# A two-layer graph kernel: the last product as seven products of halves, in a new order of steps

## The chip, the cores and the metric

The kernel runs on one core of a Trainium2 chip. The metric is the device time of one launch in microseconds (us), the median of three runs; the profile is taken by the hardware profiler in one further execution.

## The reference, cut to what matters

There are 128 graphs of 128 nodes with 512 features (`x`, f32) and a 0/1 adjacency `adj`. Two layers follow each other; each normalizes, runs an attention over the nodes of its graph and adds the result to `x`. Layer 0 has eight heads of 64, layer 1 four heads of 64. The change is in the end of layer 1:

```
# layer 0
h = relu(layernorm(x))
m = h @ map_w.T + map_b               # heads n = m / |m| per head
q = m @ q_w.T + q_b ; k = m @ k_w.T + k_b
adj0 = (n n^T > 0.1) * softmax(mask(q k^T / 8))
x = x + relu((adj0 @ (h @ gcn_map_w.T + gcn_b)) @ gcn_W.T / (adj0.sum + 1))
# layer 1
h = relu(layernorm(x))
q, k, v = h @ Wq, h @ Wk, h @ Wv      # 512 -> 256
o = softmax(mask(q k^T / 8)) @ v      # 128 x 256 per graph
x = x + o @ Wo + bo                   # 256 -> 512
```

All arithmetic is f32.

## The kernel before

**Blocks and turns.** Two graphs make a block (`G = 2`, 64 blocks). Each block goes through some forty steps, methods of `Block`. Their order is written out by hand in two lists. `TURN` (lines 934 to 1074) is one turn of the loop at line 1473: an entry `(back, step, ...)` runs the step on block `turn - back`, so that one turn works on blocks in several stages: loads and the first normalization three and two blocks ahead (back -3, -2, -1), the products of layer 0 on the block itself (0), its scores and attention one turn later (1), the mix and the products of layer 1 two turns later (2), the scores of layer 1 (3), and the last mix and the output product (4). `TAIL` (1078 to 1368) holds what is left of the last blocks; there `(back, ...)` means block 64 - back. Each engine executes its instructions in the order of these lists; waits between engines come from the data and from the reuse of buffers. For the turns before turn 2 a variant `early` of the list moves one step, `halves` of layer 0, to a place ahead of `unit 0` (lines 1469 to 1471).

**Products by halves.** The big products multiply the features of both graphs by a weight matrix. A weight matrix is cut into four blocks, the activations of the two graphs into four quarters, and instead of eight products of blocks, seven are made (`p`, lines 375 to 414), with sums of activations (`halves`, S1 to S4, on POOL; on DVE in layer 1 for the last two blocks, where `late` is true) and sums of weights made once. The seven write into three PSUM banks X, Y and Z: products 1 and 2 into X, 6, 7 and 4 into Y, 5 and 3 into Z. Between them the banks are read: `r` copies X after product 1, `u 1` reads Y after product 6, `u 2` reads Y after product 7, `c` reads a bank into the destination. So product 7 waits for `u 1`, product 4 for `u 2`, product 3 for `c 1 1`, which reads Z after product 5. The kinds are `qk` and `ms` (layer 0) and `qk1` and `v` (layer 1). `ms` streams 512 columns in each matmul, `qk`, `qk1` and `v` 128. Every f32 matmul shows as two records of PE.

**The output product.** It is not made in this way: `project(g)` (910 to 921) takes the two 128x128 pieces of `oT` (one graph's `o`, turned) as stationary operand and streams the 512 columns of `w_o1`, so four matmuls of 512 columns in a block, and `project_out` (923 to 926) adds the bank to `x1` on DVE; `store` writes `x1` out. `x1` is the block's x of layer 1 with the bias `b_o` already in it (`bias1`, POOL).

**PE's modes.** The scores use 64 rows of the array (`scores0`, `near`, `scores1` through line 557; called *row steps* below), the mixes 64 columns (`mix0` line 692, `mix1` line 892; *column steps*), the products the full array. A turn's PE steps before, with [back]:

```
mix0 0[2], mix1[4], mix0 1[2] | scores0 0[1], scores0 1[1] | p qk 1, 6, project 1[4],
p qk 2, 7, project 0[4], p qk 5, 4, 3 | scores1[3], near 1[1], near 0[1] | p ms 1, 6, 5,
p qk1 1[2], p ms 7, 2, 4, 3, p qk1 6, p v 1, 6, p qk1 7, 2, 5, p v 2, 7, p qk1 4, 3, p v 5, 4, 3
```

**Other steps that are named below.** `mix0_out` (DVE) divides the mix, `residual` adds it to x (POOL; DVE when late), `stats1`, `rstd`, `norm1` normalize (DVE, POOL, ACT), `h1`, `h1_put`, `h1_get`, `h1_out` turn the result by way of DRAM (late: by PE transposes), `squares`, `norms`, `unit`, `nT` make the unit heads (ACT, DVE, POOL, DVE), `h0_out` (ACT) writes `hT`, the input of the next block's products. `scores0_out`, `max0`, `near_out`, `scores1_out` are DVE, `exps0`, `exps1`, `near_T_out`, `mix1_out` are ACT.

Of the kernel before, what the change touches and what calls it, by code (L numbers as in the profile page):

```python
# [8 lines left out]
F32 = mybir.dt.float32  # L9
# [11 lines left out]
def kernel(  # L21
# [53 lines left out]
    w_o1 = const.tile([P, IC, D], F32, name="w_o1")  # L75
    b_ms = const.tile([P, 2, D], F32, name="b_ms")
    b_d = const.tile([P, D], F32, name="b_d")
# [146 lines left out]
    class Block:  # L224
# [130 lines left out]
        def quarters(self, layer):  # L355
            h = self.h1T if layer else self.hT
            return [[h[:, g, 2 * k : 2 * k + 2, :] for k in range(2)] for g in range(G)]

        def halves(self, layer):
            A = self.quarters(layer)  # L360
            add = (nc.vector if self.late and layer else nc.gpsimd).tensor_tensor
            tag = f"halves{layer}"
            t = keep1.tile([P, 4, 2, S], F32, tag=tag, name=f"{tag}_{self.b}")
            S1, S2, S3, S4 = (t[:, i] for i in range(4))
# [13 lines left out]
        def p(self, kind, i):  # L378
            layer = int(kind in ("qk1", "v"))
# [12 lines left out]
            if kind in ("ms", "v"):  # L392
                for c in range(2):
                    rhs = (w_ms if kind == "ms" else w_v1)[:, w, c, :]
# [5 lines left out]
                        stop=(c == 1),  # L400
# [16 lines left out]
        def dest(self, kind, g, half):  # L417
# [4 lines left out]
            if kind == "v":  # L422
                if "v1" not in f:
                    f["v1"] = keep2.tile([P, G, INNER], F32, tag="v1", name=f"v1_{b}")
                return f["v1"][:, g, half * P : (half + 1) * P]
            n = KC if kind == "qk" else IC
# [5 lines left out]
        def shaped(self, kind, t):  # L432
            if kind == "ms":
                return t.rearrange("p (k h d) -> p k h d", k=2, d=DK)
            if kind == "v":
                return t[:, :P]
            t = t.rearrange("p (c t) -> p c t", t=S)
# [4 lines left out]
        def r(self, kind, i):  # L442
            X = self.f[kind, "X"]
            if kind in ("qk1", "v"):
# [6 lines left out]
            if i == 1 and kind == "ms":  # L451
                nc.vector.tensor_add(r, X, b_ms[:, 1])
            elif i == 1:
# [5 lines left out]
            elif kind == "ms":  # L459
                nc.gpsimd.tensor_tensor(  # L460
                    self.f[kind, tag],
                    self.f[kind, "r1"],
                    self.shaped(kind, b_d),
                    ALU.add,
                )
# [8 lines left out]
        def u(self, kind, i):  # L474
            Y = self.shaped(kind, self.f[kind, "Y"])
            nc.vector.tensor_add(self.dest(kind, i - 1, 1), Y, self.f[kind, "r1"])  # L476

        def c(self, kind, g, half):
            bank = self.shaped(kind, self.f[kind, ("XZ", "YZ")[g][half]])
            out = self.dest(kind, g, half)  # L480
            if half:
# [428 lines left out]
        def project(self, g):  # L910
            b = self.b
            py = mm_bank(f"py_{b}_{g}")
            for c in range(IC):
                nc.tensor.matmul(  # L914
                    py,
                    lhsT=self.f["oT"][:, g, c, :],
                    rhs=w_o1[:, c, :],
                    start=(c == 0),
                    stop=(c == IC - 1),
                )  # L920
            self.f["py", g] = py

        def project_out(self, g):
            b = self.b
            y = self.x1[:, g, :]
            nc.vector.tensor_add(y, self.f["py", g], y)
# [8 lines left out]
        (2, "mix0", 0),  # L935
        (4, "mix1"),
        (2, "mix0", 1),
        (2, "mix0_out", 0),
        (2, "residual", 0),
        (1, "scores0", 0),  # L940
        (4, "mix1_out"),
        (1, "nT_put"),
        (1, "scores0", 1),
        (2, "mix0_out", 1),
        (2, "residual", 1),
        (0, "p", "qk", 1),
        (2, "stats1", 0),
        (2, "rstd", 1, 0),
        (1, "scores0_out", 0),
        (0, "r", "qk", 1),  # L950
        (2, "stats1", 1),
        (2, "norm1", 0),
        (0, "p", "qk", 6),
        (4, "project", 1),
        (2, "rstd", 1, 1),
        (0, "p", "qk", 2),
        (1, "max0", 0),
        (0, "u", "qk", 1),
        (0, "p", "qk", 7),
        (4, "project", 0),  # L960
        (1, "nT_get"),
        (2, "norm1", 1),
        (-2, "stats0", 1),
        (2, "bias1", 0),
        (2, "h1"),
        (0, "p", "qk", 5),
        (2, "h1_put"),
        (1, "scores0_out", 1),
        (0, "r", "qk", 2),
# [559 lines left out]
```

## Time and profile before

| | before |
|---|---|
| median of three runs | 3009.96 us (3009.82 to 3010.53) |
| the profiled execution, its own time | 3010.06 us |
| its span in the trace | 3008.3 us |
| mean granted TensorE clock | 0.999 |
| one turn in the steady state | 45.71 us |
| steady turns (4 to 62), start to end of the stretch | 199.3 to 2896.1 us |

A turn's length is read off the timeline of PE: the first scores of a turn start at 202.21, 247.92, 293.63 us and so on. In the lists of the profile, a line of a group gives line, engine, operation, output<-input, shapes and count, then busy time, mean ns of one, and idle time before it with what ended it. In a timeline, the columns are start (us), duration (us), engine, line, operation and count; an instruction's duration holds the drain of the pipeline, so a group's cost is the start of the next group minus its own start.

### The profile page before, as it was taken

The numbers are of one execution on the slowest core, as the hardware profiler recorded it, in microseconds if no ns is written. First come the engines' busy times: TensorE is split into PE (matmuls) and PEld (weight loads), VectorE is DVE, ScalarE is ACT, GpSimd is POOL, SyncE is SP. The second block draws the span as 40 slices with busy tenths as digits, with TensorE's granted clock in tenths as the row PEclk, the third lists the DMA queues.
The fourth block names the chain that finished last, engine by engine and source line by source line (L and its number), as shares of the span: only waits on it lengthen the run. The fifth ranks groups of instructions, "written<-read, shape, count | busy, mean of one in ns | idle before, by whom it ended". The sixth has DMA issues, their size and how long they took to land.

```text
span 3008.3 us, 68541 instructions
## 1 busy us (share of the span) xinstructions
PE 2986.0 (99%) x25336; PEld 2367.4 (79%) x25336; DVE 2418.2 (80%) x4586; ACT 1469.3 (49%) x4637; POOL 1750.9 (58%) x2423
## 2 busy tenths in 40 slices
PE   8999999999999999999999999999999999999999
PEld 5787787787787887877877877877878878778777
DVE  3788888888888888888888888888888888888877
ACT  2454554554544544545545545545445445455444
POOL 1566566566565565665665665655655656656642
PEclk9999999999999999999999999999999999999999
DMA  4356565565565565565555664664655655655542
GB/s 156 97 172 184 158 189 178 155 190 179 151 193 177 154 187 176 167 184 165 181 183 155 187 181 152 189 183 148 191 177 159 185 172 173 184 159 187 173 139 76
DMA packets 304109, 507.33 MB, mean 169 GB/s; under 512 B 49184, under 2 KB 180512, under 8 KB 295840
## 3 DMA queue, kind: packets, MB, share of 16 engines
q1 hardware_dynamic: 301072, 502.39, 54.8%
q8 instruction: 201, 3.29, 0.4%
q10 hardware_dynamic: 2704, 0.57, 0.1%
q14 instruction: 132, 1.08, 0.1%
HBM read 273.20 MB, written 229.64 MB: 167 GB/s over the span
## 4 chain that ended last, share of the span: by engine, by line
PE 97%; DVE 1%; DMA 1%; POOL 0%; issue 0%; ACT 0%; ACTq 0%; SPq 0%; DVEq 0%; POOLq 0%
PE py_qk L407 17%; PE px_qk L407 11%; PE pz_qk L407 11%; PE py_ms L395 11%; PE px_ms L395 8%; PE pz_ms L395 7%; PE py L914 7%; PE po L692 4%; PE psc L557 4%; PE pc L557 4%; PE py_v L395 3%; PE ps L557 2%; PE pz_v L395 2%; PE px_v L395 2%; PE po L892 2%; PE pw_k L132 0%
## 5 line engine op out<-in xcount | busy, mean ns | idle before, releaser
L617 ACT ACTIVATE s<-s,mx 128x128 f32<-128x128 f32 x1024 | 396.4, 393 | 73.0 <-DVE mx L603 73.0
L513 POOL TENSOR_TENSOR rn<-rn,mhalf 128x8 f32<-128x8 f32 x128 | 212.9, 1663 | 331.7 <-DVE rn L508 259.5
L407 PEld LDWEIGHTS py_qk<-halves,w_qk 128*128 128x128 f32 x3072 | 368.9, 192 | 32.8 <-issue 31.8
L407 PEld LDWEIGHTS pz_qk<-halves,w_qk 128*128 128x128 f32 x3072 | 368.2, 192 | 29.4 <-issue 28.7
L407 PE MATMUL py_qk<-halves,w_qk 128*128 128x128 f32 x3072 | 387.3, 276 | 2.3 <-DVE kT L476 2.2
L407 PE MATMUL pz_qk<-halves,w_qk 128*128 128x128 f32 x3072 | 385.0, 275 | 0.4 <-DVE halves L365 0.4
L407 PEld LDWEIGHTS px_qk<-hT,w_qk 128*128 128x128 f32 x2048 | 243.9, 192 | 39.7 <-issue 32.3
L365 POOL TENSOR_TENSOR halves<-h1T 128x256 f32<-128x256 f32 x62 | 45.0, 726 | 381.2 <-ACT h1T L318 381.2
L407 PE MATMUL px_qk<-hT,w_qk 128*128 128x128 f32 x2048 | 256.5, 279 | 3.5 <-DVE mix L713 3.5
L815 ACT ACTIVATE s<-s,mx 128x128 f32<-128x128 f32 x496 | 192.9, 390 | 136.2 <-DVE mx L802 136.2
L395 PE MATMUL px_ms<-w_ms,hT 128*128 128x512 f32 x512 | 247.1, 605 | 0.0
L914 PE MATMUL py<-w_o,oT 128*128 128x512 f32 x512 | 240.9, 594 | 0.9 <-DVE oT L905 0.9
L395 PE MATMUL py_ms<-w_ms,halves 128*128 128x512 f32 x512 | 240.7, 592 | 0.0
L395 PE MATMUL pz_ms<-w_ms,halves 128*128 128x512 f32 x512 | 240.6, 592 | 0.0
L318 ACT ACTIVATE hT<-mv 128x1024 f32<-128x1024 f32 x64 | 67.7, 1057 | 318.1 <-PE py_ms L395 318.1
L456 ACT ACTIVATE r_qk<-px_qk,b_k 128x128 f32<-128x128 f32 x256 | 73.2, 369 | 271.1 <-PE px_qk L407 271.1
L724 POOL TENSOR_TENSOR x<-x,mix 128x512 f32<-128x512 f32 x124 | 157.3, 1269 | 71.2 <-DVE mix L713 55.7
L617 ACT ACTIVATION_READ_ACCUMULATOR s<-s,mx 128x1 f32 x1024 | 197.1, 193 | 0.0
L851 POOL TENSOR_TENSOR s<-s,z 128x512 f32<-128x512 f32 x124 | 126.3, 1040 | 118.6 <-DVE z L844 118.6
L395 PEld LDWEIGHTS pz_ms<-w_ms,halves 128*128 128x128 f32 x512 | 97.2, 190 | 122.0 <-issue 107.4
L395 PEld LDWEIGHTS px_ms<-w_ms,hT 128*128 128x128 f32 x512 | 91.9, 189 | 98.9 <-issue 91.4
L395 PEld LDWEIGHTS py_ms<-w_ms,halves 128*128 128x128 f32 x512 | 92.5, 190 | 92.8 <-issue 92.5
(151 smaller groups left out, 7196.1 us busy)
## 6 DMA issues: line engine op xcount, KB each, us to landing
d_h<-hn SPq DMA_DIRECT2D x504, 128.0 KB, 3.7
mv<-d_h SPq DMA_DIRECT2D x126, 512.0 KB, 4.3
d_near<-s SPq DMA_DIRECT2D x248, 256.0 KB, 3.8
near_mv<-d_near SPq DMA_DIRECT2D x62, 1024.0 KB, 5.4
xt<-in_x SPq DMA_DIRECT2D x64, 512.0 KB, 7.2
x<-in_x SPq DMA_DIRECT2D x64, 512.0 KB, 6.3
out<-x SPq DMA_DIRECT2D x128, 256.0 KB, 2.3
d_n<-n SPq DMA_DIRECT2D x248, 128.0 KB, 3.0
```

The source lines that it names most:

```text
L318: nc.scalar.activation(t.rearrange("p g c (a j) -> p (g c) a j", a=Q), self.f.pop((key, "moved")).rearrange("p a r j -> p r a j"), func,)
L395: nc.tensor.matmul(bank[:, : rhs.shape[1]], lhsT=src[:, c, :], rhs=rhs, start=(first and c == 0), stop=(c == 1), skip_group_check=True,)
L407: nc.tensor.matmul(bank[:, oc * P : (oc + 1) * P], lhsT=(w_qk1 if layer else w_qk)[:, w, c, oc * P : (oc + 1) * P], rhs=src[:, c, :], star ...
L456: nc.scalar.activation(r[:, cols], X[:, cols], AF.Identity, bias=b_k[:, oc : oc + 1])
L513: nc.gpsimd.tensor_tensor(rn, rn, mhalf[:, :H0], ALU.pow)
L557: nc.tensor.matmul(dst[par][:, :, first + step * p, :], lhsT=lT(rows, p), rhs=rT(rows, p), start=True, stop=True,)
L617: nc.scalar.activation(s[:, :, g, par, c, :], s[:, :, g, par, c, :], AF.Exp, bias=mx[:, i : i + 1], accum_out=z[:, h : h + 1],)
L692: nc.tensor.matmul(po[h // PR][half * DK : (half + 1) * DK, h % PR, :], lhsT=f["nearT", g][:, (h % 2) * PR + h // 2, half * DK : (half + 1 ...
L724: (nc.vector if self.late else nc.gpsimd).tensor_add(x1, x1, self.f["mix", g])
L815: nc.scalar.activation(s[:, :, par, c, g, :], s[:, :, par, c, g, :], AF.Exp, bias=mx[:, par, c, g : g + 1], accum_out=z[:, par, c, g : g + 1],
L851: nc.gpsimd.tensor_tensor(s[:, :, par].rearrange("p q c g j -> p q (c g) j"), s[:, :, par].rearrange("p q c g j -> p q (c g) j"), z[:, par ...
L914: nc.tensor.matmul(py, lhsT=self.f["oT"][:, g, c, :], rhs=w_o1[:, c, :], start=(c == 0), stop=(c == IC - 1),)
```

## The change

The product with `w_o` becomes a fourth user of the seven products (kind `y`, "layer" 2): the quarters are the 128x128 pieces of `oT`, the weight blocks 128x256, and each product is one matmul of 256 columns. `halves 2` makes the four sums of `oT` (POOL; DVE when late) in the buffer that `halves 1` uses; `r y` copies product 1 to SBUF (ACT); `first_to_x1` adds that copy to the three quarters of `x1` that need it (POOL, 128x256 and 128x512); then two `u` and four `c` add the banks to quarters of `x1` in place (DVE, 128x256 each). `project` and `project_out` go. `w_o1` is loaded by four transfers instead of one, and its four sums are made by DVE in the first turns, where the pieces of such work (`one_piece`) are now also spread over the `qk` steps. The constant `b_d` goes; `r ms 2` becomes two POOL additions over contiguous operands instead of one. Both lists have a new order. The turn's PE steps after it:

```
mix0 0[2], mix0 1[2], mix1[4] | scores0 0[1] | p qk 1, 6 | scores0 1[1], scores1[3] |
p qk 2, 7, 5, 4, 3 | near 1[1], near 0[1] | p ms 1, p y 1[4], p ms 6, 5, p y 6, p ms 7,
p y 5, 7, 2, p qk1 1[2], p ms 2, p y 3, 4, p ms 4, 3, p qk1 6, p v 1, 6, 5, p qk1 7, 5,
p v 7, p qk1 2, p v 2, p qk1 4, p v 3, p qk1 3, p v 4
```

`h0_out` now stands after `squares 1` and `unit 0`, and in the early turns `halves` of layer 0 stands behind `h0_out`, and so behind `unit 0`. `nT_put` moves from the next turn to the end of its own.

The diff, its two lists cut:

```diff
@@ -72,9 +72,8 @@
     w_qk = const.tile([P, 7, 2, D], F32, name="w_qk")
     w_qk1 = const.tile([P, 7, 2, INNER], F32, name="w_qk1")
     w_v1 = const.tile([P, 7, 2, INNER // 2], F32, name="w_v1")
-    w_o1 = const.tile([P, IC, D], F32, name="w_o1")
+    w_o1 = const.tile([P, 7, 1, D // 2], F32, name="w_o1")
     b_ms = const.tile([P, 2, D], F32, name="b_ms")
-    b_d = const.tile([P, D], F32, name="b_d")
     b_o = const.tile([P, D], F32, name="b_o")
     b_q = const.tile([P, KC], F32, name="b_q")
     b_k = const.tile([P, KC], F32, name="b_k")
@@ -353,15 +352,18 @@
 
 
         def quarters(self, layer):
+            if layer == 2:
+                return [[self.f["oT"][:, g, k : k + 1, :] for k in range(IC)] for g in range(G)]
             h = self.h1T if layer else self.hT
             return [[h[:, g, 2 * k : 2 * k + 2, :] for k in range(2)] for g in range(G)]
 
         def halves(self, layer):
             A = self.quarters(layer)
             add = (nc.vector if self.late and layer else nc.gpsimd).tensor_tensor
-            tag = f"halves{layer}"
-            t = keep1.tile([P, 4, 2, S], F32, tag=tag, name=f"{tag}_{self.b}")
-            S1, S2, S3, S4 = (t[:, i] for i in range(4))
+            t = keep1.tile(
+                [P, 4, 2, S], F32, tag=f"halves{min(layer, 1)}", name=f"halves{layer}_{self.b}"
+            )
+            S1, S2, S3, S4 = (t[:, i, : 1 if layer == 2 else 2] for i in range(4))
             add(S1, A[1][0], A[1][1], ALU.add)
             add(S2, S1, A[0][0], ALU.subtract)
             add(S3, A[0][0], A[1][0], ALU.subtract)
@@ -376,7 +378,7 @@
 
 
         def p(self, kind, i):
-            layer = int(kind in ("qk1", "v"))
+            layer = {"qk1": 1, "v": 1, "y": 2}.get(kind, 0)
             A = self.quarters(layer)
             S = self.f.get(("S", layer))
             nm, src, w, first = (
@@ -389,15 +391,17 @@
                 ("Y", S and S[2], T3, False),
             )[i - 1]
             bank = self.parts(kind, nm)
-            if kind in ("ms", "v"):
-                for c in range(2):
-                    rhs = (w_ms if kind == "ms" else w_v1)[:, w, c, :]
+            if kind in ("ms", "v", "y"):
+                weights = {"ms": w_ms, "v": w_v1, "y": w_o1}[kind]
+                n = weights.shape[2]
+                for c in range(n):
+                    rhs = weights[:, w, c, :]
                     nc.tensor.matmul(
                         bank[:, : rhs.shape[1]],
                         lhsT=src[:, c, :],
                         rhs=rhs,
                         start=(first and c == 0),
-                        stop=(c == 1),
+                        stop=(c == n - 1),
                         skip_group_check=True,
                     )
                 return
@@ -423,6 +427,8 @@
                 if "v1" not in f:
                     f["v1"] = keep2.tile([P, G, INNER], F32, tag="v1", name=f"v1_{b}")
                 return f["v1"][:, g, half * P : (half + 1) * P]
+            if kind == "y":
+                return self.x1[:, g, half * HD : (half + 1) * HD]
             n = KC if kind == "qk" else IC
             nm = (("qT", "kT") if kind == "qk" else ("q1", "k1"))[half]
             if nm not in f:
@@ -434,6 +440,8 @@
                 return t.rearrange("p (k h d) -> p k h d", k=2, d=DK)
             if kind == "v":
                 return t[:, :P]
+            if kind == "y":
+                return t[:, :HD]
             t = t.rearrange("p (c t) -> p c t", t=S)
             return t[:, : KC if kind == "qk" else IC]
 
@@ -441,6 +449,10 @@
 
         def r(self, kind, i):
             X = self.f[kind, "X"]
+            if kind == "y":
+                self.f["y", "r1"] = r = keep1.tile([P, D], F32, tag="n2", name=f"p1_{self.b}")[:, :HD]
+                nc.scalar.copy(r, self.shaped(kind, X))
+                return
             if kind in ("qk1", "v"):
                 self.f[kind, "r1"] = self.f[kind, "r2"] = r = self.dest(kind, 0, 0)
                 nc.scalar.copy(r, self.shaped(kind, X))
@@ -450,6 +462,7 @@
             self.f[kind, tag] = self.shaped(kind, r)
             if i == 1 and kind == "ms":
                 nc.vector.tensor_add(r, X, b_ms[:, 1])
+                self.f["ms", "p1"] = r
             elif i == 1:
                 for oc in range(KC):
                     cols = slice(oc * P, (oc + 1) * P)
@@ -457,12 +470,8 @@
                         r[:, cols], X[:, cols], AF.Identity, bias=b_k[:, oc : oc + 1]
                     )
             elif kind == "ms":
-                nc.gpsimd.tensor_tensor(
-                    self.f[kind, tag],
-                    self.f[kind, "r1"],
-                    self.shaped(kind, b_d),
-                    ALU.add,
-                )
+                nc.gpsimd.tensor_tensor(r, self.f["ms", "p1"], b_ms[:, 1], ALU.subtract)
+                nc.gpsimd.tensor_tensor(r, r, b_ms[:, 0], ALU.add)
             else:
                 nc.gpsimd.tensor_tensor(
                     self.f[kind, tag],
@@ -473,12 +482,13 @@
 
         def u(self, kind, i):
             Y = self.shaped(kind, self.f[kind, "Y"])
-            nc.vector.tensor_add(self.dest(kind, i - 1, 1), Y, self.f[kind, "r1"])
+            out = self.dest(kind, i - 1, 1)
+            nc.vector.tensor_add(out, Y, out if kind == "y" else self.f[kind, "r1"])
 
         def c(self, kind, g, half):
             bank = self.shaped(kind, self.f[kind, ("XZ", "YZ")[g][half]])
             out = self.dest(kind, g, half)
-            if half:
+            if half or kind == "y":
                 nc.vector.tensor_add(out, bank, out)
             elif g:
                 nc.vector.tensor_add(out, bank, self.f[kind, "r2"])
@@ -907,23 +917,15 @@
                 nc.scalar.copy(oT, self.f["po1"])
             self.f["oT"] = oT
 
-        def project(self, g):
-            b = self.b
-            py = mm_bank(f"py_{b}_{g}")
-            for c in range(IC):
-                nc.tensor.matmul(
-                    py,
-                    lhsT=self.f["oT"][:, g, c, :],
-                    rhs=w_o1[:, c, :],
-                    start=(c == 0),
-                    stop=(c == IC - 1),
-                )
-            self.f["py", g] = py
-
-        def project_out(self, g):
-            b = self.b
-            y = self.x1[:, g, :]
-            nc.vector.tensor_add(y, self.f["py", g], y)
+
+        def first_to_x1(self, g):
+            r = self.f["y", "r1"]
+            if g:
+                x1 = self.x1[:, 1, :].rearrange("p (i c) -> p i c", i=2)
+                r = r[:, None, :].broadcast_to([P, 2, HD])
+            else:
+                x1 = self.dest("y", 0, 1)
+            nc.gpsimd.tensor_tensor(x1, x1, r, ALU.add)
 
         def store(self, g):
             nc.sync.dma_start(out=out[self.b * G + g], in_=self.x1[:, g, :])
     TURN = (
         (2, "mix0", 0),
+        (2, "mix0", 1),
         (4, "mix1"),
+        (2, "mix0_out", 0),
+        (1, "scores0", 0),
...
+        (0, "p", "qk", 1),
...
+        (0, "p", "qk", 6),
+        (2, "stats1", 0),
+        (1, "scores0", 1),
...
+        (3, "scores1"),
...
+        (4, "halves", 2),
...
+        (0, "p", "qk", 3),
+        (1, "near", 1),
+        (1, "exps0", 1, 0),
+        (1, "near", 0),
+        (0, "p", "ms", 1),
...
+        (4, "p", "y", 1),
...
+        (4, "first_to_x1", 0),
+        (4, "p", "y", 6),
+        (4, "u", "y", 1),
...
+        (0, "p", "ms", 3),
...
+        (0, "c", "ms", 0, 1),
+        (0, "squares", 0),
+        (2, "p", "v", 6),
+        (-2, "norm0", 1),
...
+        (2, "c", "v", 1, 1),
...
+        (0, "unit", 0),
+        (-1, "h0_out"),
+        (2, "p", "v", 3),
...
+        (2, "p", "v", 4),
...
+        (0, "unit", 1),
...
+        (-1, "halves", 0),
+        (0, "nT"),
+        (0, "nT_put"),
...
     TAIL = (
...
+        (2, "mix0", 0),
...
+        (2, "mix0", 1),
+        (2, "mix0_out", 0),
...
+        (2, "mix0_out", 1),
...
+        (1, "scores0_out", 0),
...
+        (1, "max0", 0),
...
+        (2, "residual", 1),
+        (2, "residual", 0),
...
+        (2, "stats1", 1),
...
+        (1, "scores0_out", 1),
...
+        (1, "max0", 1),
...
+        (4, "p", "y", 6),
+        (2, "stats1", 0),
+        (4, "p", "y", 2),
+        (3, "scores1_out"),
+        (4, "c", "y", 0, 0),
+        (2, "rstd", 1, 0),
+        (1, "near_out", 1),
+        (4, "first_to_x1", 0),
+        (4, "u", "y", 1),
+        (4, "p", "y", 7),
...
+        (2, "p", "qk1", 1),
...
+        (1, "mix0", 0),
...
+        (1, "mix0_out", 0),
+        (1, "mix0", 1),
+        (1, "mix0_out", 1),
...
+        (1, "residual", 1),
...
+        (1, "h1_out"),
...
+        (1, "scores1"),
+        (1, "scores1_out"),
+        (2, "mix1"),
+        (2, "mix1_out"),
+        (2, "halves", 2),
...
+        (1, "exps1", 0),
...
+        (1, "mix1_out"),
+        (1, "p", "y", 1),
+        (1, "r", "y", 1),
+        (2, "c", "y", 1, 0),
+        (1, "halves", 2),
...
+        (1, "c", "y", 0, 0),
         (1, "store", 0),
     )
@@ -1419,7 +1494,12 @@
         load_ms()
         ahead(0, "h0_get")
         ahead(1, "load")
-        load_weights(w_o1, wo)
+        for i in range(IC):
+            for j in range(2):
+                nc.sync.dma_start(
+                    out=w_o1[:, BLOCKS[i][j], 0],
+                    in_=wo[i * P : (i + 1) * P, j * HD : (j + 1) * HD],
+                )
         for i in range(2):
             rows = slice(i * HD, (i + 1) * HD)
             for j in range(2):
@@ -1453,10 +1533,9 @@
         nc.vector.tensor_add(b_k, pb[:, :KC], bk_col)
         nc.vector.tensor_sub(b_qk, b_q, b_k)
         sums_of_weights(w_ms)
-        nc.vector.tensor_sub(b_d, b_ms[:, 0], b_ms[:, 1])
         later = [("scale", w_qk1, w) for w in (B11, B21)]
-        later += [("sub", w, *sum) for w in (w_qk1, w_v1) for sum in SUMS]
+        later += [("sub", w, *sum) for w in (w_qk1, w_v1, w_o1) for sum in SUMS]
         def one_piece():
             op, w, o, *ab = later.pop(0)
@@ -1468,14 +1547,14 @@
         halves = (-1, "halves", 0)
         early = [t for t in TURN if t != halves]
-        early.insert(early.index((0, "unit", 0)), halves)
+        early.insert(early.index((-1, "h0_out")) + 1, halves)
         for turn in range(1 + min(t[0] for t in TURN), NB - 1):
             for back, step, *args in early if turn < 2 else TURN:
                 b = turn - back
                 if 0 <= b < NB and (b, step, *args) not in done:
                     getattr(block(b), step)(*args)
-                    if later and turn >= 0 and step in ("u", "c") and args[0] == "ms":
+                    if later and turn >= 0 and step in ("u", "c") and args[0] in ("qk", "ms"):
                         one_piece()
             blocks.pop(turn - 4, None)
         for back, step, *args in TAIL:
```

## The prediction

> **What bounds the kernel now.** I read the page's busy times and its chain of waits first, then the busy times by stretches, then the timeline of PE in one steady turn and in the last turns.
>
> ```profile
> PE 2986.0 (99%) x25336; PEld 2367.4 (79%) x25336; DVE 2418.2 (80%) x4586; ACT 1469.3 (49%) x4637; POOL 1750.9 (58%) x2423
> ...
> PE 97%; DVE 1%; DMA 1%; POOL 0%; issue 0%; ACT 0%; ACTq 0%; SPq 0%; DVEq 0%; POOLq 0%
> ```
>
> PE ends nearly every step of the chain. By stretches (PE, PEld, DVE, ACT, POOL):
>
> ```profile
> 50.20:156.70 106.50, 99.47 (x722) 77.16 (x721) 75.06 (x132) 39.63 (x120) 52.09 (x73) 0.98 0.30 90
> ...
> 199.30:2896.10 2696.80, 2696.80 (x23129) 2148.79 (x23128) 2212.11 (x4184) 1344.85 (x4247) 1622.95 (x2237) 1.00 0.57 174
> 2896.10:3008.30 112.20, 105.23 (x953) 82.22 (x952) 82.81 (x181) 50.05 (x179) 39.98 (x55) 0.99 0.28 90
> ```
>
> The middle holds 59 turns of 45.71 us in which PE never idles: there the price is what PE executes. In the first turns and the last 112 us PE idles 7 us each: there the price is what PE waits for. So I sum three parts. A steady turn's PE, start to start:
>
> ```profile
> 1523.65 0.61 PE L395 MATMUL py_v<-w_v,h1T 128*128 128x128 f32 x4
> 1524.20 0.71 PE L395 MATMUL pz_v<-w_v,halves 128*128 128x128 f32 x4
> 1524.84 1.16 PE L692 MATMUL po<-ms,s 128*64 128x66 f32 x32
> 1525.83 1.04 PE L892 MATMUL po<-aT,v 128*64 128x128 f32 x16
> 1526.70 1.11 PE L692 MATMUL po<-ms,s 128*64 128x66 f32 x32
> 1527.74 2.06 PE L557 MATMUL psc<-kT,qT 64*128 64x128 f32 x32
> 1529.72 2.05 PE L407 MATMUL px_qk<-hT,w_qk 128*128 128x128 f32 x16
> 1531.61 1.95 PE L407 MATMUL py_qk<-halves,w_qk 128*128 128x128 f32 x16
> 1533.40 1.88 PE L914 MATMUL py<-w_o,oT 128*128 128x512 f32 x4
> 1535.12 1.95 PE L407 MATMUL px_qk<-hT,w_qk 128*128 128x128 f32 x16
> ```
>
> **Steady turn, the output product.** One `project` costs 1535.12 - 1533.40 = 1.72, both 3.44. Seven products of 256 columns are not in the trace. Half of a 512-column matmul is 0.43; as two 128-column ones (a `v` product, 0.45 a group elsewhere in the turn, exactly 0.447) it is 0.447. I take 0.432, near the wide row, since a weight load has twice the time of the 128-column stream: 3.02, a gain of 0.42.
>
> The records say 429 ns for 512 columns and four times 111.7 = 447 ns for four of 128, so three more records cost 18 ns, 6 ns each. The Trainium skill ("TensorEngine Tiling (Array Packing)", Instruction Overhead) speaks against the change: about 60 cycles of overhead in each matmul, at the 2.4 GHz of its clock page 25 ns; by that, 14 records for 8 would return 0.15 us a turn, 9 us in all. The rows decide.
>
> **One more row step.** Before, five score steps stand in two places of a turn, after it in three: `scores0 0`, then `p qk 1, 6`, then `scores0 1, scores1`, then five products, then both `near`. What leaving and coming back costs is seen alone in the last turns:
>
> ```profile
> 2904.80 1.88 PE L914 MATMUL py<-w_o,oT 128*128 128x512 f32 x4
> 2906.61 1.16 PE L557 MATMUL ps<-k,q 64*128 64x128 f32 x16
> 2907.70 2.05 PE L407 MATMUL py_qk<-halves,w_qk 128*128 128x128 f32 x16
> 2909.59 1.95 PE L407 MATMUL px_qk<-hT,w_qk 128*128 128x128 f32 x16
> ```
>
> The group before it takes 1.81 for 1.72, the 16 score records 1.09, the group behind it 1.89 for 1.79. Two steps together (`psc` above) take 1.98, so 16 records cost 0.89 and the excursion 0.09 + 0.20 + 0.10 = 0.4. One more a turn: **+0.40**, as much as the product saves.
>
> **One wait less.** `p v 3` starts 0.55 after `p v 4` (1523.65 to 1524.20), where such a group takes 0.45: it waits for `c v 1 1`, which ends at 1524.14. It then takes 0.64, of which 0.09 is the way into column mode and 0.10 the refilled pipeline. After the change `p v 5` comes early and `c v 1 1` ends 1.4 us ahead of `p v 3`: -0.20. The three mixes in their new order cost 0.99 + 0.99 + 0.97 for 0.99 + 0.87 + 1.04: +0.05.
>
> **What the other engines take.** These rows price the adds:
>
> ```profile
> L926 DVE TENSOR_TENSOR x<-py,x 128x512 f32<-128x512 f32 x128 | 87.8, 686 | 65.1 <-PE py L914 65.1
> ...
> L482 DVE TENSOR_TENSOR k<-pz_qk,k 128x256 f32<-128x256 f32 x128 | 54.3, 424 | 61.5 <-PE pz_qk L407 61.5
> ...
> L366 POOL TENSOR_TENSOR halves<-halves,hT 128x256 f32<-128x256 f32 x64 | 47.2, 738 | 5.0
> ```
>
> DVE gives two of 0.69 and gets six of 0.42: 37.5 + 1.1 = 38.6 of 45.5 us. POOL gets four `halves 2` (0.46 each, from 0.74 for 256 and 1.27 for 512 columns; bounds 0.23, an `rstd` row, and 0.74), 0.73 + 1.27 for `first_to_x1` and 1.27 for the second part of `r ms 2`: 27.5 + 5.1 = 32.6. ACT gets 0.37 (its copy of `q`). All this is beside PE as long as no product comes too early. I followed each reuse of a bank or buffer: the nearest are `p qk1 7` behind `u qk1 1` (0.2 + 0.69 + 0.42 + 0.41 = 1.7 after `p ms 3`, PE has 0.89 + 3 x 0.45 = 2.2 to do: 0.5 spare), `mix0 1` behind `near_T_out 1` (0.7 spare, since `mix1` no longer stands between the mixes) and `halves 1`, whose buffer `p y 3` now holds (2.4 spare). `h1` moves back on DVE; from its end to `h1T` takes 9.5 us before (1491.2 to 1500.7) and about 2 remain ahead of `p qk1 1`. On SP, `h0_put` now stands behind `nT_put`, which waits for `nT`; both get steps still have over 2 us. The added queues carry no transfer of y. If the cover of one such wait goes, it costs 0.2, as `p v 3` shows.
>
> A steady turn: -0.42 + 0.40 - 0.20 + 0.05 = -0.17; 59 of them **-10.0**.
>
> **First turns.** In turn 0, DVE loses the 0.68 of `b_d` ahead of `u qk 1`, for which PE waits 1.55: -0.7. At turn 1, with T the end of `p ms 3`, `h0_out` stands behind `squares 0`, `norm0`, `squares 1` on ACT: 0.2 + 0.69 + 0.63 + 0.80 + 0.63, so it ends at T + 4.1 (before: 76.2, T - 0.4). `halves` stands behind `unit 0`, which waits for `norms 0` (T + 2.5) and takes 2.85: its second sum is there at T + 6.8, and `p qk 6` starts then instead of T + 4.0. PE still owes one score step and its excursion (1.3), and a wait of 0.3 goes: +3.8. At turn 2, PE waits twice now:
>
> ```profile
> PE px_qk L407 <- DVE mix L713: 3.5, 1, 3.5
> ```
>
> and 1.6 for ACT before that, and the next two products take 2.6 for 1.79 (the granted clock of that stretch is 0.98, 1.00 later). After the change the first mix stands behind `h0_out` and `norm0` (+6.0 after the last product, 4 us idle), and DVE's `nT` behind the later `unit 1` ends at 12.4, `mix0_out 0` at 14.2, `u qk 1` at 20; `p ms 1` comes at 29.8 where it was 28.15: +1.6. Turn 3 has the row step without the product's gain: +0.2. Sum **+4.9**.
>
> The slow products behind the long wait are what the skill's "TensorE: Matmul & The Clock Gate" (Part 1) calls the clock gate, which closes after an idle window of about 3.4 us; by it the wait of 2.9 at turn 1 would be free of it and that of 4 at turn 2 not.
>
> **Last turns.** Stretches between PE steps, before from the timeline, after by sums of rows: to block 62's `mix0` 45.6, then 46.0 (+0.4). From there to its `p qk1 1` 17.7, then: DVE starts 1.2 later with two `mix0_out` (1.5), four score and maximum steps (1.2), two residuals (0.68), two `stats1` (0.9), `scores1_out` 2.6, `c y 0 0`, `near_out 1` 1.2, `u y 1`, 15.6 in all, so `p y 7` starts at 16.8, where PE has only 10.6 of work; four y products and two transposes (1.0 each) follow: 20.6 (+2.9). To the end of block 63's mixes 13.1, then 12.7 (-0.4). To its transposes 5.7, then 7.6, as `mix0_out 0` no longer runs before the second mix (+1.9). To the end of its scores 12.9, then 14.5, with two y and two v products moved in (+1.6). To the end of the span 17.2, then 19.3: `project` and one add were 4.5, and a ladder of sums, product, add, product, four adds takes its place (+2.1). Sum **+8.5**.
>
> Total: -10.0 + 4.9 + 8.5 = +3.4 on the profiled execution's 3010.06 (0.1 above the median): **3013.5**.
>
> **Rivals.** *The edges cost nothing*: waits in the first and last turns trade places and only the steady turns count, 3010.1 - 10.0 = 3000. For it: the lists are long and PE idles 14 us there already; against it: `halves` is plainly behind `unit 0`. *A new wait in each steady turn* (the other side): DVE comes over 0.5 us late at `u qk1 1`, `p qk1 7` stops for 0.2, 59 x 0.2 = 11.8, 3025. For it: six more DVE instructions, three just ahead of it; against it: DVE waits for PE there. *256 columns cost as two of 128*, so the product saves less than it says: 7 x 0.015 x 59 = 6.2, 3019.7.
>
> **Numbers.** Forecast 0.42, edges free 0.24, new wait 0.22, dear columns 0.12. 0.2% (6 us, about what a measurement of this kernel can tell from no change) reaches from 3004 to 3016: that is the likeliest case's own range, so same 0.42, faster 0.24, slower 0.34. The range takes in the first and the second rival: 2999 to 3025.
>
> **What would show it.** Steady turns of 45.54; a y product of 0.43; three score groups a turn with 1.09, 1.98, 1.98; `p v` 4 to the mix in 0.54; `p qk 6` of turn 1 some 6.8 after the last `ms` product; an idle PE of 6 us ahead of a y product in the last 70 us. A steady turn at 45.3 or below, or at 45.7, would make the forecast wrong.

## The result and the profile after

The changed kernel takes 3016.4 us (median of 14 runs, 3015.7 to 3017.7) against 3009.9 for the kernel before on the same chip: a ratio of 1.0021, 95% interval 1.0013 to 1.0029. It is 6.5 us slower, just over the 6 us up to which the prediction called a change the same. The forecast was 3013.5, its range 2999 to 3025; of its three outcomes "same" had 0.42, and "slower", which came by half a microsecond, 0.34. Its profiled execution took 3015.85, with a span of 3014.1.

The page of the kernel after, busy times:

```profile
PE 2975.5 (99%) x25720; PEld 2441.0 (81%) x25720; DVE 2492.7 (83%) x4853; ACT 1436.8 (48%) x4701; POOL 2060.5 (68%) x2863
```

PE executes 10.5 us less than before, and still the kernel is longer: the gain lies where PE is always busy, the loss where it waits. The stretches (their length, PE, PEld, DVE, ACT, POOL busy, then the granted clock) show it:

```profile
49.88:162.40 112.52, 102.75 (x722) 80.08 (x720) 76.33 (x134) 39.79 (x120) 56.72 (x76) 0.95 0.27 79
...
204.00:2886.70 2682.70, 2682.70 (x23483) 2213.73 (x23482) 2272.46 (x4421) 1310.63 (x4306) 1909.38 (x2650) 1.00 0.59 175
2886.70:3014.10 127.40, 107.47 (x983) 88.62 (x982) 95.36 (x211) 51.84 (x184) 57.24 (x78) 0.96 0.27 84
```

The 59 steady turns take 2682.7 for 2696.8: **-14.1**. They begin at 204.0 for 199.3: **+4.7**. The last turns take 127.4 for 112.2: **+15.2**, 20 us of it without PE work where there were 7, and at a lower clock. The sum is +5.8, the difference of the spans.

A steady turn of the kernel after, on PE (start, duration, operation; what a group costs is the next start minus its own):

```profile
1476.62 0.61 PE L399 MATMUL py_v<-w_v,h1T 128*128 128x128 f32 x4
1477.16 2.09 PE L702 MATMUL po<-ms,s 128*64 128x66 f32 x64
1479.08 1.04 PE L902 MATMUL po<-aT,v 128*64 128x128 f32 x16
1480.06 1.16 PE L567 MATMUL psc<-kT,qT 64*128 64x128 f32 x16
...
1484.92 1.16 PE L567 MATMUL psc<-kT,qT 64*128 64x128 f32 x16
1485.91 1.06 PE L567 MATMUL ps<-k,q 64*128 64x128 f32 x16
...
1503.70 0.59 PE L399 MATMUL py_y<-w_o,halves 128*128 128x256 f32 x2
1504.13 1.88 PE L399 MATMUL py_ms<-w_ms,halves 128*128 128x512 f32 x4
```

A `y` product costs 1504.13 - 1503.70 = 0.43. There is no `p v 3` that waits ahead of the mixes any more: `p v 4` to the mix is 0.54. The three mixes cost 1477.16 to 1480.06 = 2.90, as before (1524.84 to 1527.74). The row steps stand in three places. A turn is 45.47 for 45.71.

In turn 1 and in the last 70 us PE waits, and then it is slow:

```profile
75.70 1.16 PE L567 MATMUL psc<-kT,qT 64*128 64x128 f32 x16
79.54 3.79 PE L411 MATMUL px_qk<-hT,w_qk 128*128 128x128 f32 x16 [2.68 <-ACT hT L317]
83.12 3.21 PE L411 MATMUL py_qk<-halves,w_qk 128*128 128x128 f32 x16
...
2949.43 1.22 PE L399 MATMUL py_y<-w_o,halves 128*128 128x256 f32 x2 [4.42 <-DVE x L486]
2950.44 1.06 PE L399 MATMUL pz_y<-w_o,halves 128*128 128x256 f32 x2
2951.30 1.85 PE L295 MATMUL pt<-ident,hn 128*128 128x128 f32 x8
```

The bracket is the wait and what ended it. Behind the 2.68 two products take 3.58 and 3.14 for their usual 1.79; the granted clock of that stretch, in the view of windows, says why:

```profile
79.50:86.30 6.80, 6.76 (x34) 6.64 (x34) 3.60 (x5) 3.63 (x15) 6.56 (x10) 0.54 0.64 164
```

The mean clock is 0.54 there, and 0.69 behind the 4.42 (2949.40 to 2955.10), where it is 1.00 in the steady turns.

### The profile page after: what moved, and what is told of

The parts are those of the page before. It is cut to its first block, busy times and chain, and to the rows that moved or that the text cites. A ratio compares the mean times of both kernels' runs of the same rounds, so it can differ in the third digit from the quotient of the medians.

```text
span 3014.1 us, 70045 instructions
## 1 busy us (share of the span) xinstructions
PE 2975.5 (99%) x25720; PEld 2441.0 (81%) x25720; DVE 2492.7 (83%) x4853; ACT 1436.8 (48%) x4701; POOL 2060.5 (68%) x2863
## 4 chain that ended last, share of the span: by engine, by line
PE 97%; DVE 1%; DMA 1%; POOL 0%; issue 0%; ACT 0%; ACTq 0%; DVEq 0%; SPq 0%; POOLq 0%
PE py_qk L411 17%; PE px_qk L411 12%; PE pz_qk L411 11%; PE py_ms L399 11%; PE px_ms L399 8%; PE pz_ms L399 7%; PE psc L567 4%; PE pc L567 4%; PE po L702 4%; PE py_v L399 3%; PE py_y L399 3%; PE px_v L399 2%; PE pz_v L399 2%; PE ps L567 2%; PE pz_y L399 2%; PE po L902 2%
## 5 line engine op out<-in xcount | busy, mean ns | idle before, releaser
L507 ACT ACTIVATE n<-ms 128x512 f32<-128x512 f32 x128 | 80.6, 630 | 432.2 <-DVE ms L492 390.5
L411 PE MATMUL px_qk<-hT,w_qk 128*128 128x128 f32 x2048 | 264.1, 282 | 2.7 <-ACT hT L317 2.7
L627 ACT ACTIVATION_READ_ACCUMULATOR s<-s,mx 128x1 f32 x1024 | 208.1, 203 | 0.0
L331 POOL TENSOR_SCALAR rstd<-mv 128x1 f32<-128x1 f32 x256 | 57.5, 225 | 193.7 <-DVE mv L196 184.3
L928 POOL TENSOR_TENSOR x<-x,p 128x256 f32<-128x256 f32 (+1 forms) x128 | 125.9, 1005 | 90.0 <-ACT p L454 90.0
L651 DVE SCALAR_TENSOR_TENSOR s<-pc,s 128x512 f32<-128x512 f32 x256 | 163.5, 680 | 4.5 <-PE pc L567 4.5
L603 DVE TENSOR_TENSOR s<-psc,neg 128x512 f32<-128x512 f32 x256 | 163.4, 679 | 0.0
```

What stands on the lines that cost most here:

```text
L411: nc.tensor.matmul(bank[:, oc * P : (oc + 1) * P], lhsT=(w_qk1 if layer else w_qk)[:, w, c, oc * P : (oc + 1) * P], rhs=src[:, c, :], star ...
L507: nc.scalar.activation(n2.rearrange("p (h d) -> p h d", d=DK), mss[:, 0, g, :, :DK], AF.Square)
L603: nc.vector.tensor_add(f["s"][:, :, g, par], f["psc", g][par], neg[:, :, None, :].broadcast_to([P, Q, PR, SQ]),)
L627: nc.scalar.activation(s[:, :, g, par, c, :], s[:, :, g, par, c, :], AF.Exp, bias=mx[:, i : i + 1], accum_out=z[:, h : h + 1],)
L651: nc.vector.scalar_tensor_tensor(sp, cp, 0.1, sp, ALU.is_gt, ALU.mult,)
L928: nc.gpsimd.tensor_tensor(x1, x1, r, ALU.add)
```

## The experiments

The theory after the result: the product, the third row group and the missing wait have the prices that were forecast, and only the first and last turns differ from it, where waits and the clock behind them were under-priced. The rival: the steady turn came out right by errors that cancel. Marks of each profiled execution in us: start of the third group of `mix0` (where the 59 turns begin), length of a turn, last stretch (from the end of the 59 turns on); the time is the median of 4 to 16 runs.

| kernel | time | start | turn | last |
|---|---|---|---|---|
| before | 3009.9 to 3010.2 | 199.2 | 45.71 | 112.2 |
| after | 3016.4 | 204.0 | 45.47 | 127.4 |
| wait_away | 3007.5 | 199.8 | 45.66 | 112.2 |
| wait_away_copy_ahead | 2999.2 | 198.7 | 45.51 | 112.4 |
| order_alone | 3035.7 | 206.4 | 45.88 | 120.5 |
| product_alone | 3238.0 | 197.9 | 49.2 | 133.8 |
| rows_joined | 2990.2 | 201.2 | 45.08 | 128.5 |
| y_split | 3022.7 | 204.2 | 45.58 | 127.7 |
| early_moved | 3012.0 | 199.3 | 45.47 | 129.2 |
| tail_of_before | 3001.0 | 204.3 | 45.47 | 112.1 |
| first_on_dve | 3014.7 | 204.1 | 45.47 | 127.4 |
| joined_early_tail | 2973.2 | 199.7 | 45.08 | 112.6 |

**The wait at p v 3.** The kernel before, its turn's list alone edited:

```diff
+        (2, "p", "v", 5),
         (2, "p", "v", 7),
         (2, "p", "qk1", 4),
         (2, "u", "v", 2),
+        (2, "c", "v", 1, 1),
         (2, "p", "qk1", 3),
-        (2, "p", "v", 5),
...
         (2, "p", "v", 4),
-        (2, "c", "v", 1, 1),
```

> The kernel before, with p v 5 moved ahead of p v 7 and c v 1 1 right behind u v 2, in the turn's list alone. Theory (p v 3 waits 0.1 for c v 1 1 and refills the pipeline in 0.1): p v 4 to the first mix falls from 1.19 (1523.65 to 1524.84) to about 0.99, a steady turn from 45.71 to 45.51, 59 of them give -11.8, 2998. Rival: the wait only moves to the next PE step (a mix that waits for near_T_out instead), a steady turn stays at 45.71 and the time at 3010.

It gave 0.9991 (0.9982 to 1.0000) and a turn of 45.66: 0.05, not 0.2. The rival held. In the timeline of wait_away, ACT's copy of `near` ends where the mix starts:

```profile
1523.01 1.05 ACT L678 COPY s<-near_mv 128x1024 f32<-128x1024 f32 x1
...
1523.42 0.61 PE L395 MATMUL pz_v<-w_v,halves 128*128 128x128 f32 x4
...
1524.11 1.16 PE L692 MATMUL po<-ms,s 128*64 128x66 f32 x32
```

The copy runs to 1524.06, and `p v 3` to the mix is 0.69. On ACT it stands behind `c qk1 0 0`, which it doesn't need and which waits for DVE. So a second edit moved it:

```diff
+        (1, "near_T_out", 0),
         (2, "c", "qk1", 0, 0),
-        (1, "near_T_out", 0),
```

> The kernel wait_away (before, with p v 5 and c v 1 1 early) and near_T_out 0 moved ahead of c qk1 0 0 on ACT, so that the first mix has nothing left to wait for. Theory (the wait of 0.1 and the refill of 0.1 were worth 0.2 a turn, and in wait_away the mix took it over from p v 3, because the copy of near stood behind a sum on ACT): a steady turn of 45.51, 59 x 0.2 = -11.8 against before, 2998. Rival (only the wait was worth anything, the way into column mode costs 0.2 by itself): a steady turn of 45.6 or more, 3004 or more.

0.9963 (0.9950 to 0.9975), a turn of 45.51: the theory. So the 0.2 of the forecast was real, but two releases stood behind it. The list after makes both moves (`near_T_out 0` stands ahead of both `c qk1 0`), and the forecast named only the first.

**The order without the product.** The lists of after, with `project 1` for `p y 1`, `project 0` for `p y 7`, the two `project_out` for `c y 1 1` and `c y 0 1`; the other `y` steps left out, and the code of the kernel before otherwise.

```diff
-        (4, "p", "y", 1),
+        (4, "project", 1),
-        (4, "p", "y", 7),
+        (4, "project", 0),
-        (4, "c", "y", 1, 1),
+        (4, "project_out", 1),
-        (4, "c", "y", 0, 1),
+        (4, "project_out", 0),
```

> The orders of the kernel after (turn, first turns and last turns) with the product in four wide matmuls (project 1 at the place of p y 1, project 0 at that of p y 7, the two adds at those of c y 1 1 and c y 0 1). Theory: a steady turn is 45.47 + 0.42 = 45.89, 59 of them +10.6; the first turns lengthen by 5 as in the kernel after, since halves 0 still stands behind unit 0; of the 15 us of the last turns the order has 6 to 10 and the ladder of the product the rest: 3032 to 3036. Rival (the ladder alone lengthens the last turns): last turns within 3 us of the 112 before, 3026 to 3028.

1.0085 (1.0071 to 1.0099), and the time, the turn and the last turns are as expected: a turn of 45.88, so that the product saves 45.88 - 45.47 = **0.41** in this order, and last turns of 120.5. The first turns were not: the start is at 206.4, 7.2 later than before, for the 5 expected; its clock is at 0.50 from 130.25 to 137.08, where that of after is 1.00. Of the 15.2 of the last turns the order has 8.3, and the remaining 6.9 come with the seven products.

**The product without the order.** The steps of `y` near the places of `project` and `project_out` in the lists of before:

```diff
         (0, "p", "qk", 6),
-        (4, "project", 1),
+        (4, "p", "y", 1),
+        (4, "r", "y", 1),
+        (4, "first_to_x1", 0),
...
         (0, "p", "qk", 7),
-        (4, "project", 0),
+        (4, "p", "y", 6),
+        (4, "u", "y", 1),
...
```

> The seven products of halves in the orders of the kernel before (each y step near the place of the project or project_out that it replaces), turn and last turns. Theory: a steady turn is 45.71 - 0.42 = 45.29 (the wait at p v 3 stays, no third row group), 59 of them give -24.8; the first turns -0.7; the last turns lengthen by the ladder of sum, copy, product and add of the last blocks, 4 to 8 us: 2989 to 2993. Rival (the product costs as much as it saves, 7 x 0.447 and new waits for its sums): a steady turn of 45.5 or more, 3005 or more. If the last turns lengthen by less than 3 us, the ladder is not what lengthened them in the kernel after.

1.0755 (1.0740 to 1.0770): neither. This doesn't price the product, since the places that I chose made new waits. The timeline of product_alone in one turn, DVE and PE:

```profile
1541.21 0.42 DVE L486 TENSOR_TENSOR x<-py_y,x 128x256 f32<-128x256 f32 x1 [2.98 <-PE py_y L399]
...
1544.82 0.68 DVE L486 TENSOR_TENSOR kT<-py_qk,r_qk 128x512 f32<-128x512 f32 x1
...
1545.55 2.05 PE L411 MATMUL py_qk<-hT,w_qk 128*128 128x128 f32 x16 [1.80 <-DVE kT L486]
```

`u y 1` waits 2.98 for its product, DVE's queue stands behind it, and `u qk 2` comes so late that PE stops for 1.80. The product does need a place where DVE doesn't wait for it, as between the `ms` products.

**The third row group.** The kernel after, its turn's list alone edited:

```diff
         (1, "scores0", 0),
+        (1, "scores0", 1),
...
-        (1, "scores0", 1),
...
-        (3, "scores1"),
...
-        (3, "scores1_out"),
         (0, "p", "qk", 3),
+        (3, "scores1"),
         (1, "near", 1),
+        (3, "scores1_out"),
```

> The kernel after, with scores0 1 put beside scores0 0 and scores1 beside near 1 again (scores1_out behind near 1), so that a turn has two groups of 32 and 48 row-step records in place of three. Theory (leaving the normal mode and coming back costs 0.40 each time): a steady turn falls from 45.47 to 45.07, 59 x 0.40 = -23.6, and the first turns by about 1: 2992. Rival (the excursion is priced elsewhere, for example in the first group after the mixes, or the later scores1_out makes PE wait for attn_get at the end of the turn): a steady turn of 45.4 or more, 3012 or more.

0.9934 (0.9921 to 0.9948), a turn of 45.08: 45.47 - 45.08 = **0.39** for one more excursion, in every turn. This is also the product in the row groups of before without the wait: 45.71 - 0.42 - 0.20 = 45.09. With order_alone and the pair of wait_away runs it rules out the rival of cancelling errors.

**The record.** The kernel after, each product of 256 columns issued as two of 128 in `p`:

```diff
-                for c in range(n):
-                    rhs = weights[:, w, c, :]
-                    nc.tensor.matmul(bank[:, : rhs.shape[1]], lhsT=src[:, c, :], rhs=rhs,
+                width = P if kind == "y" else weights.shape[3]
+                for c in range(n):
+                    for at in range(0, weights.shape[3], width):
+                        nc.tensor.matmul(bank[:, at : at + width], lhsT=src[:, c, :],
+                            rhs=weights[:, w, c, at : at + width],
...
```

> The kernel after, with each product of 256 columns issued as two of 128 (14 more instructions of the program in a turn, 28 more records). Theory (a record costs some 6 ns beyond its columns, as 447 against 429 ns for 512 columns): a product takes 0.447 in place of 0.432, a steady turn 45.47 + 0.105 = 45.58, 59 of them +6.2, and 0.1 to 0.5 in the edges: 3023. Rival by the Trainium skill (TensorEngine Tiling (Array Packing), Instruction Overhead, some 60 cycles, 25 ns, for each): 14 x 2 x 25 ns = 0.7 us a turn, 3058. A second rival (nothing, the stream of columns alone counts): 45.47, 3016.

A turn of 45.58 and 3022.7, 6.3 over after: the theory. The expectation counted the records wrongly: a product has two records and gets four, so a turn has 7 more instructions and 14 more records. 0.105 / 14 = 7.5 ns each, near the 6 ns of the forecast. By the 60 cycles (25 ns) of the expectation for each of 14 an estimate is 0.35 us a turn, over three times what was measured. (What the Trainium skill, "TensorEngine Tiling (Array Packing)", Instruction Overhead, says beside that figure, that one column takes as long as 60, is no addition to a stream of 128, and the run agrees with this.)

**The first turns.** The kernel after:

```diff
-        early = [t for t in TURN if t != halves]
-        early.insert(early.index((-1, "h0_out")) + 1, halves)
+        h0_out = (-1, "h0_out")
+        early = [t for t in TURN if t not in (halves, h0_out)]
+        first = early.index((0, "squares", 0))
+        early[first:first] = [h0_out, halves]
```

> The kernel after; in the list of the first turns alone h0_out stands ahead of squares 0 and halves 0 right behind it, ahead of unit 0, as in the kernel before. Theory (in turn 1 PE waits 2.7 for hT, runs two products at half the clock for it, 3.1, and turn 2 begins late by the same chain): turn 1 falls from 35.76 to about 30.5 and turn 2 by 0.5 to 1, start of turn 4 from 204.0 to about 198: 3010 to 3011. Rival (the copy of h0 comes late by its transfer, since h0_get stands later in the list, and not by its place on ACT): turn 1 stays above 34 and the time above 3014.

1.0007 (0.9998 to 1.0015) against before, 4.4 less than after; the 59 turns begin at 199.3, as before the change (198 was expected). The first product of turn 1 starts at 76.76 and takes 1.89, with no wait. So the first turns' loss is the place of `h0_out` and `halves 0`. The last stretch, in which nothing was edited, took 1.8 longer, at a clock of 0.92 for 0.96.

**The last turns.** The kernel after, with the order of the last turns of before (less its `nT_put`, which the new turn has done already) and the wide product there:

```diff
+        nc.vector.tensor_add(w_o1[:, T1], w_o1[:, T1], w_o1[:, B11])
         for back, step, *args in TAIL:
...
+                for j in range(2):
+                    nc.tensor.matmul(py[:, j * HD : (j + 1) * HD],
+                        lhsT=self.f["oT"][:, g, c, :], rhs=w_o1[:, BLOCKS[c][j], 0, :],
```

> The kernel after; the last turns in the order of the kernel before and with the wide product there (two matmuls of 256 columns in place of each of 512, since B12 is put back into the place of T1 by one addition). Theory (the 15 us of the last turns come from their order and from the ladder of the seven products, which nothing covers there): the last turns take 112 to 114 in place of 127.4, 3001 to 3003. Rival (what the new turn leaves unfinished on DVE and POOL at its end makes the last turns longer whatever their list): 118 or more, 3007 or more.

0.9971 (0.9960 to 0.9983), the last stretch 112.1: all of the 15.2 is in the list and the product of the last turns, nothing in what the new turn leaves behind.

**A part of the ladder.** In the last 20 us of the kernel after, DVE's second half sum takes 1.24 for 0.28 beside POOL's `first_to_x1`, and PE waits 2.81 for it:

```profile
2994.65 2.00 POOL L928 TENSOR_TENSOR x<-x,p 128x256 f32<-128x256 f32 x2 [12.49 <-ACT p L454]
...
2995.56 1.24 DVE L368 TENSOR_TENSOR halves<-halves,oT 128x128 f32<-128x128 f32 x1
```

So the add was moved to DVE there:

```diff
-            nc.gpsimd.tensor_tensor(x1, x1, r, ALU.add)
+            (nc.vector if self.late else nc.gpsimd).tensor_tensor(x1, x1, r, ALU.add)
```

> The kernel after; first_to_x1 of the last two blocks runs on DVE, in its place in the list (behind halves 2), where it ran on POOL beside DVE's halves. Theory (DVE's second half sum took 1.24 for 0.28, and another 0.81, because POOL's add ran at the same time): these take 0.28 again, y product 6 of block 62 waits 1.8 in place of 2.81, the clock stays up and the four products behind it take 0.43 in place of 0.58 to 0.95; from the end of block 63's scores to the end of the span 19 to 20.5 in place of 22.3: 3013 to 3014.5. Rival (the half sum waits for something of its own, a landing of mix1_out's second copy): 1.24 stays, and DVE's two adds, now behind the halves, make it 0 to 1 slower: 3016 to 3018.

The half sum takes 0.29 and the wait is 1.79, as the theory had it. The time is 3014.7 (1.7 less, ranges that meet) and the last stretch the same 127.4: from the end of block 63's scores it is 1.1 shorter, and ahead of them 1.1 longer, by another slow clock, which after did not have at this place. In the timeline of first_on_dve:

```profile
2975.78 1.09 PE L295 MATMUL pt<-ident,hn 128*128 128x128 f32 x8 [2.01 <-ACT hn L283]
...
2977.26 1.93 PE L411 MATMUL px_qk<-h1T,w_qk 128*128 128x128 f32 x8
```

The second line's group usually costs 0.89 to 0.98; here the next starts 1.73 later. The products behind the wait of 1.79 were slow as well, so the part of the expectation that the clock would stay up was wrong.

**Together.** The edits of rows_joined, early_moved and tail_of_before in one kernel:

> The three edits of rows_joined, early_moved and tail_of_before together. Theory (each acts in a stretch of its own, so the gains add): 3016.4 - 26 - 6 - 14 = 2970, with a steady turn of 45.08. Rival (scores1_out stands later in the joined turn, and the last turns of before then wait for it): over 2980.

0.9876 (0.9861 to 0.9892): 2973.2, 36.8 less than before and 43.2 less than after, and 3 short of the sum: rows_joined's gain of 26 held 2.8 in the first turns (its 59 turns begin at 201.2 for 204.0), and early_moved takes that same wait away by itself. The scores that stand later don't hold up the last turns: the last stretch is 112.6.

## Why the prediction was right, and where it was not

- **Steady turn.** Forecast -0.42, +0.40, -0.20, +0.05; measured -0.41 (order_alone), +0.39 (rows_joined), -0.20 (the pair of wait_away) and 0 for the mixes. The last term was mis-sized: 0.99 + 0.99 + 0.97 was reckoned from single groups, and the new order of three takes 2.90 as the old one did. The sum is -0.22 and the turn shows -0.24; 59 turns give -14.1 for -10.0.
- **The total.** +5.8 between the spans for +3.4. Against the forecast the steady turns gave 4.1 more, the first turns 0.2 more, and the last turns cost 6.7 more. That the time lies 2.9 over the forecast and not 7 is luck: the error of the steady turns hides part of that of the last.
- **Rivals.** "A new wait in each steady turn" didn't come: PE's idle time in the 59 turns is 0. product_alone shows what such a wait costs where it does come (1.80 a turn and more). "256 columns cost as two of 128" is refuted: 0.43, and 0.45 when they are issued so (y_split). "The edges cost nothing" is refuted by 20 us.
- **First turns.** +4.7 for +4.9, by errors that cancel. Turn 0 gave -1.0 for -0.7. Turn 1 cost +5.6 for +3.8. With T at 75.6, `px_qk` starts with `hT` at T + 3.9, for T + 4.1, and in the timeline of POOL the second half sum ends at 82.59, T + 7.0, for T + 6.8: these steps of the prediction held. The step that failed is that the two products behind the wait were priced at full speed. At half the clock `px_qk` ends only at 83.12, T + 7.5, and `p qk 6`, which then starts, takes 3.14 for 1.79: 0.5 and 1.35, the 1.8 that are missing. In rows_joined (T at 75.8), where the clock stayed up, `p qk 6` starts at T + 7.0 and waits for that sum:

```profile
79.74 2.05 PE L411 MATMUL px_qk<-hT,w_qk 128*128 128x128 f32 x16 [1.79 <-ACT hT L317]
82.84 2.05 PE L411 MATMUL py_qk<-halves,w_qk 128*128 128x128 f32 x16 [1.05 <-POOL halves L368]
```

  Turn 2 gave +1.2 up to `p ms 1`, for +1.6, and -0.2 behind it; turn 3 gave -0.9 for +0.2, in part since PE waited 0.40 for `kT` there before (at 166.96) and doesn't now; the sum left this out.
- **Last turns.** +15.2 for +8.5. By its six stretches: +0.3, +4.4, -0.4, +2.6, +3.1, +5.1 for +0.4, +2.9, -0.4, +1.9, +1.6, +2.1. The direction was right in each, and order_alone and tail_of_before put 8.3 on the order and 6.9 on the product; the sizes of the second, fourth, fifth and sixth were not right. The step that failed in the second and sixth is that the products behind a wait were priced at full speed. In the second `p y 7` starts 16.84 behind block 62's `mix0`, as forecast (16.8), after an idle of 4.4 (6 was forecast); what follows takes 1.01, 0.86 and 1.69 for 0.43, 0.43 and 0.87: 1.8 more, where the stretch is 1.5 over its forecast. In the sixth, where "a ladder of sums, product, add, product, four adds" was put at +2.1, five products took 4.05 for 2.15, and the half sum was held for 0.96: together 2.9, where the stretch is 3.0 over. The 1.5 that the fifth is over have two parts. PE is busy 0.8 longer than forecast (three `y` products stand in it, not two), and it idles 1.54 for 0.76 before, in three waits for DVE (0.59, 0.27, 0.67, in the timeline of PE); the prediction put no new wait there. DVE's second and third half sum take 1.40 and 1.49 for 0.41 while POOL adds `b_o`:

```profile
2979.49 2.67 POOL L744 TENSOR_TENSOR x<-x,b_o 128x512 f32<-128x512 f32 x2
...
2979.64 1.40 DVE L368 TENSOR_TENSOR halves<-halves,h1T 128x256 f32<-128x256 f32 x1
```

  This is what the sums of the last 20 us show too; no run took this add away. Why the fourth is 0.7 over stays open.
- **The clock.** The prediction set the long wait of turn 2 against a page on the clock. By the Trainium skill ("TensorE: Matmul & The Clock Gate", Part 1) the clock falls after an idle window of some 3.4 us that runs freely; read as a threshold for one wait, it freed the wait of turn 1. The runs contradict that reading. Behind 2.68 the clock fell; behind a wait of 1.79 in rows_joined's turn 1 it stayed at 1.00, and 58 waits of 1.8 to 2.1 in product_alone, each in a busy turn, left it at 1.00 too; behind 2.01 it fell in first_on_dve and not in rows_joined; behind 1.79 in the thin last 20 us it fell. No single length of wait decides. The record of the clock in the traces shows what the falls go with. The granted clock is 1.00 or 0.50 (0.54 and 0.69 are means of stretches with both), and its falls in one execution lie whole multiples of 3.413 us apart (in after 78.94, 116.49, 2946.14 and 2997.34: 11, 829 and 15 steps). Cut on this grid, into cells of 3.41 us, the two waits of 2.01 look as follows, first in rows_joined, then in first_on_dve (columns as in the stretches above):

```profile
2946.13:2949.55 3.42, 2.03 (x20) 1.45 (x18) 3.22 (x9) 1.21 (x3) 2.78 (x8) 1.00 0.00 0
2949.55:2952.96 3.41, 2.79 (x21) 2.47 (x22) 2.29 (x6) 1.85 (x4) 3.34 (x4) 1.00 0.00 0
...
2973.60:2977.01 3.41, 1.40 (x11) 1.13 (x10) 2.97 (x7) 2.17 (x4) 3.17 (x6) 1.00 0.02 5
2977.01:2980.42 3.41, 3.41 (x14) 2.88 (x12) 1.18 (x3) 0.92 (x3) 3.20 (x4) 0.50 0.00 0
```

  In rows_joined the wait is divided between two cells of the grid, with PE busy for 2.03 and 2.79; in first_on_dve it lies in one, with 1.40, and the next cell is at 0.50. Counted over the twelve traces, between PE's first and last matmul: all 31 cells at full clock with PE busy for under 42% are followed by one at 0.50, none of those with over 56% is, and of the 56 between four are.

What stays open: how much of the 15.2 of the last turns is the clock alone. The rows above give 3.7 in two stretches. The record of the clock gives about the same as an estimate: of the last turns 10.2 us are at 0.50 (2946.14 to 2952.97 and 2997.34 to 3000.75), PE is busy for 6.9 of them, and half of that is 3.5. What such a delay sets off further on isn't in it; a run that keeps the waits and holds the clock up wasn't made.

## What to carry to other kernels

Price a change apart for the stretches in which the bounding engine is always busy and for those in which it waits: here the first gained 14 us by plain sums of rows, and the ends gave back 20. A scheme that trades matmul columns for sums on other engines lengthens the chain at the ends, and a wait there can be paid twice (behind 2.7 us of it two products took 3.0 longer, and the turn lost 1.8), so keep the plain product there, as tail_of_before does. A wait that is removed is worth its price only when every release of the step behind it is early, so look for the one that stands second.

## What was not expected of the hardware

- An excursion into row mode of one group costs 0.39 us in a busy turn, as much as 230 columns of a fp32 product (0.43 for 256).
- A DVE sum of two operands in SBUF (128x128, 0.28) was held to 1.24 while POOL added from SBUF at the same time, and was 0.29 with POOL idle (first_on_dve). The Trainium skill ("GPSIMD Engine Reference", Specifications) names this contention for DVE instructions with two SBUF inputs; the runs agree.
- The granted clock is 1.00 or 0.50 on a grid of 3.41 us, and it fell behind cells in which PE was busy for less than about half, not behind waits of some length: a wait of 2.01 was followed by 0.50 in first_on_dve and by 1.00 in rows_joined.
